# A selective scan on three engines: softplus of the next chunk in single steps, and five of sixteen input products moved to GpSimd

## The chip, the core and the metric

The kernel runs on one core of one Trainium2 chip. A core has five engines that run side by side, each with its own queue, worked through strictly in order: TensorE (matmul, PE in the profile; PEld is its weight load), VectorE (DVE), ScalarE (ACT), GpSimd (POOL) and SyncE (SP, which here issues most transfers). They share SBUF, the working memory of 128 partitions; TensorE writes its results to PSUM, which VectorE and ScalarE read and GpSimd does not in this kernel. The metric is device time in microseconds of one execution; lower is better. Before the change the median of three runs is 19478.2 us (19477.44 to 19488.43).

## What is computed

The reference is a two-layer network on an image of 4 × 64 × 64 positions with 128 channels. Only its first block matters here: a selective scan of an image in four directions (k = 0 to 3: by rows, by columns, and both reversed). Cut to that:

```python
x_dbl = einsum('bkdl,kcd->bkcl', xs, x_proj_weight)
dts, Bm, Cm = split(x_dbl, [R, R + N], axis=2)          # R = 8, N = 16 states
dts = einsum('bkrl,kdr->bkdl', dts, dt_projs_weight)
delta = softplus(dts + dt_projs_bias)                   # step sizes
A = -exp(A_logs)
def step(h, xs):                                        # over the 4096 positions
    ut, dt, bt, ct = xs
    dA = exp(dt[..., None] * A)
    h = dA * h + (dt * ut)[..., None] * bt[:, :, None, :]
    y = einsum('bkdn,bkn->bkd', h, ct)
    return (h, y)
```

There are 256 channels d (two halves h of 128, one channel to a partition), 16 states n, 4 directions k and 4 images b. All numbers are float32. After the scan come a normalization, a gate and a projection, then a mixture of experts, a second layer of mixing, and a long convolution by matmul.

## The kernel before

The images are worked one after the other. For each, a first part makes the convolved input xc and, by matmul, the rows of dts, B and C for all four directions, which go to a DRAM tensor xd. Then comes the scan, the part that the change touches, and then normalization and projection. Everything after the four images (experts, second layer, convolution) is not touched.

The scan of one image runs over 32 chunks: 4 directions of 8 chunks of 512 positions (SC). Directions 2 and 3 go backwards. In directions 1 and 3 (k odd) the image is read by columns, so that xc and the sum yac are accessed with a stride. In all there are 128 chunks, each like this:

- du = dl · xc (L296, VectorE, once for each half), into PSUM. dl holds the step sizes of this chunk. du has one buffer.
- For each of 16 states n: two transfers bring row n of B and of C from xd, spread over 128 partitions, into bb (L306) and cc (L310), six buffers each.
- For each half h of each state: ScalarE makes da = exp(dl · A) into PSUM (L315); VectorE makes the product db = du · bb (L319) and the scan hh from da and db (L323 backwards, L327 forwards); ScalarE copies the last column of hh to hst, with which the next chunk starts (L331); GpSimd makes hc = hh · cc (L333); TensorE adds hc to yps in PSUM by a matmul with the identity (L334; float32 takes two passes).
- At the end VectorE adds yps to yac (L338, once for each half).

The step sizes of the next chunk are made ahead, by step_sizes (L259 to L283), which is called once in a chunk, at n == 4 (L303). A transfer brings dts (L263). For each half a matmul makes dt_ps (L270), and ScalarE takes Abs of it (L274, into ex) and Relu (L275, into dl). Then for both halves at once, 1024 columns: ScalarE Exp (L276), VectorE w = ex + 1 (L277), VectorE ex = (w − 1) − ex (L279), ScalarE Ln (L280), GpSimd w − ex (L281) and dl + w (L282). Exp and Ln lie in different activation tables, so each chunk loads a table before Ln and one after it.

The tile that holds dt_ps carries the tag of da: both share the same two buffers in PSUM, in the order in which they are asked for. hh and hc have four buffers each, db two, dl two, ex and w one.

A framework places the instructions: it takes those of the program, orders each engine's queue by its own estimate, and puts in the semaphores. So the order in a queue isn't quite that of the program text. In the built kernel before, both dt_ps matmuls stand next to each other on TensorE, between the two sums of state 3, and Abs, Relu, Abs, Relu, Exp stand in one row on ScalarE.

Of the kernel before, what the change touches and what calls it, by code (L numbers as in the profile page):

```python
# [8 lines left out]
F32 = mybir.dt.float32  # L9
AF = mybir.ActivationFunctionType  # L10
ALU = mybir.AluOpType
# [4 lines left out]
P = 128  # L16
# [9 lines left out]
NCH = L // CH  # L26
SC = 512
NSC = L // SC
HALF = L // 2
TC = 512  # L30

# [2 lines left out]
def kernel(  # L34
# [35 lines left out]
    nc = tc.nc  # L70
# [53 lines left out]
    with ExitStack() as c0:  # L124
# [37 lines left out]
        for b in range(B):  # L162
# [5 lines left out]
            with tc.tile_pool(name="pa", bufs=1) as pa, tc.tile_pool(  # L168
                name="pa_ps", bufs=6, space=PSUM
# [23 lines left out]
                for g in range(8):  # L193
                    for h in range(2):
                        ps = pps.tile([P, 8, W], F32, name="cv_ps", tag="ps")
                        for t in range(9):
# [12 lines left out]
                            bias=cb[:, h : h + 1],  # L209
# [24 lines left out]
            with ExitStack() as cb_:  # L234
# [6 lines left out]
                with tc.tile_pool(name="pb", bufs=2) as pb, tc.tile_pool(  # L241
                    name="pb_ps", bufs=1, space=PSUM
                ) as bps:

                    chunks = []
                    for k in range(K):
                        for step in range(NSC):
                            chunks.append((k, step, NSC - 1 - step if k >= 2 else step))

                    def spatial(t, k, ci, h):  # L250

                        if k % 2 == 1:
                            n = SC // H
                            return t[:, h, :].rearrange("p (r w) -> p w r", w=W)[
                                :, ci * n : (ci + 1) * n, :
                            ]
                        return t[:, h, ci * SC : (ci + 1) * SC].rearrange("p (r w) -> p r w", w=W)

                    def step_sizes(k, ci):  # L259

                        cs = slice(ci * SC, (ci + 1) * SC)
                        dts = pb.tile([R, SC], F32, name="dts")
                        nc.sync.dma_start(dts, xd[k, 0:R, cs])  # L263
                        dl = pb.tile([P, 2, SC], F32, name="dl")
                        ex = pb.tile([P, 2, SC], F32, name="ex", bufs=1)
                        w = pb.tile([P, 2, SC], F32, name="w", bufs=1)

                        for h in range(2):
                            ps = bps.tile([P, SC], F32, name="dt_ps", tag="da", bufs=2)
                            nc.tensor.matmul(  # L270
                                ps, dtw[:, k, h * P : (h + 1) * P], dts, start=True, stop=True
                            )
                            bias = dtb[:, k, h : h + 1]
                            nc.scalar.activation(ex[:, h, :], ps, AF.Abs, bias=bias)  # L274
                            nc.scalar.activation(dl[:, h, :], ps, AF.Relu, bias=bias)  # L275
                        nc.scalar.activation(ex, ex, AF.Exp, scale=-1.0)  # L276
                        nc.vector.tensor_scalar(w, ex, 1.0, None, ALU.add)  # L277

                        nc.vector.scalar_tensor_tensor(ex, w, -1.0, ex, ALU.add, ALU.subtract)  # L279
                        nc.scalar.activation(w, w, AF.Ln)  # L280
                        nc.gpsimd.tensor_sub(w, w, ex)  # L281
                        nc.gpsimd.tensor_add(dl, dl, w)  # L282
                        return dl  # L283

                    ahead = step_sizes(chunks[0][0], chunks[0][2])
                    hst = None
                    for i, (k, step, ci) in enumerate(chunks):
                        rev = k >= 2
                        cs = slice(ci * SC, (ci + 1) * SC)
                        last = 0 if rev else SC - 1  # L290
                        if step == 0:
                            hst = pb.tile([P, 2, N], F32, name="hst")
                        dl = ahead
                        du = bps.tile([P, 2, SC], F32, name="du")
                        for h in range(2):
                            nc.vector.tensor_mul(  # L296
                                du[:, h, :].rearrange("p (r w) -> p r w", w=W),
                                dl[:, h, :].rearrange("p (r w) -> p r w", w=W),
                                spatial(xc, k, ci, h),
                            )  # L300
                        yps = bps.tile([P, 2, SC], F32, name="yps", bufs=2)
                        for n in range(N):
                            if n == 4 and i + 1 < len(chunks):  # L303
                                ahead = step_sizes(chunks[i + 1][0], chunks[i + 1][2])
                            bb = pb.tile([P, SC], F32, name="bb", bufs=6)
                            nc.sync.dma_start(  # L306
                                bb, xd[k, R + n : R + n + 1, cs].to_broadcast([P, SC])
                            )
                            cc = pb.tile([P, SC], F32, name="cc", bufs=6)
                            nc.sync.dma_start(  # L310
                                cc, xd[k, R + N + n : R + N + n + 1, cs].to_broadcast([P, SC])
                            )
                            for h in range(2):
                                da = bps.tile([P, SC], F32, name="da", tag="da", bufs=2)
                                nc.scalar.activation(  # L315
                                    da, dl[:, h, :], AF.Exp, scale=aneg[:, k, h, n : n + 1]
                                )
                                db = pb.tile([P, SC], F32, name="db")
                                nc.vector.tensor_mul(db, du[:, h, :], bb)  # L319
                                hh = pb.tile([P, SC], F32, name="hh", bufs=4)  # L320
                                init = 0.0 if step == 0 else hst[:, h, n : n + 1]
                                if rev:
                                    nc.vector.tensor_tensor_scan(  # L323
                                        hh[:, ::-1], da[:, ::-1], db[:, ::-1], init, ALU.mult, ALU.add
                                    )
                                else:
                                    nc.vector.tensor_tensor_scan(  # L327
                                        hh, da, db, init, ALU.mult, ALU.add
                                    )
                                if step < NSC - 1:  # L330
                                    nc.scalar.copy(hst[:, h, n : n + 1], hh[:, last : last + 1])  # L331
                                hc = pb.tile([P, SC], F32, name="hc", bufs=4)
                                nc.gpsimd.tensor_mul(hc, hh, cc)  # L333
                                nc.tensor.matmul(  # L334
                                    yps[:, h, :], ident, hc, start=(n == 0), stop=(n == N - 1)
                                )
                        for h in range(2):
                            nc.vector.tensor_add(  # L338
                                spatial(yac, k, ci, h),
                                spatial(yac, k, ci, h),  # L340
                                yps[:, h, :].rearrange("p (r w) -> p r w", w=W),
                            )


                with tc.tile_pool(name="po", bufs=2) as po, tc.tile_pool(
                    name="po_ps", bufs=2, space=PSUM
# [67 lines left out]
    with ExitStack() as c1:  # L414
# [11 lines left out]
        with ExitStack() as c2:  # L426
# [13 lines left out]
            with tc.tile_pool(name="gate", bufs=1) as gp, tc.tile_pool(  # L440
                name="gate_ps", bufs=4, space=PSUM
# [56 lines left out]
            with tc.tile_pool(name="exp", bufs=2) as ep, tc.tile_pool(  # L498
                name="exp_ps", bufs=2, space=PSUM
# [54 lines left out]
        with tc.tile_pool(name="l1", bufs=2) as lp, tc.tile_pool(  # L554
            name="l1_ps", bufs=6, space=PSUM
# [53 lines left out]
    with tc.tile_pool(name="stu_w", bufs=2) as wp:  # L609
# [38 lines left out]
        for src, acc in ((m_plus, accp), (m_minus, accm), (m_u, mu_t)):  # L648
            for i in range(4):
                n = src.shape[1]  # L650
# [17 lines left out]
    nc.vector.memset(carry, 0.0)  # L668
    for t in range(HALF // TC):
        nj = 4 * (t + 1)  # L670
# [32 lines left out]
        for k in range(KF):  # L703


            ev = fp.tile([P, HALF], F32, name="ev")
            nc.sync.dma_start(
                ev[:, 0:width],
                bass.AP(phi.tensor, phi[k, 0, HALF - width].offset, [[1, P], [1, width]]),
            )  # L710
            od = fp.tile([P, HALF + 1], F32, name="od")
            nc.sync.dma_start(
                od[:, 0 : width + 1],
                bass.AP(phi.tensor, phi[k, 1, HALF - width].offset, [[1, P], [1, width + 1]]),
            )
            for b in range(B):
                for a in range(2):
                    pe = fps.tile([P, TC], F32, name="e_ps", tag="eps")
                    po = fps.tile([P, TC], F32, name="o_ps", tag="ops")
                    for ps, slab, pa, off in ((pe, ev, a, 0), (po, od, 1 - a, 1 - a)):  # L720
                        for j in range(nj):
                            n = TC - max(0, P * (j - 4 * t))
# [46 lines left out]
def _layout(i):  # L769
# [15 lines left out]
    w2 = z["L0_ffn_weight2"]  # L785
    phi = np.zeros((KF, 2, HALF + P), f)
    for a in range(2):
# [52 lines left out]
```

## Time and profile before

| | us |
|---|---|
| median of three runs | 19478.2 |
| the profiled execution | 19460.9 |
| its span, first to last instruction | 19459.1 |
| VectorE busy in the span | 9714.3 (50%) |
| TensorE busy | 15393.0 (79%) |
| GpSimd busy | 5972.1 (31%) |
| ScalarE busy | 4733.9 (24%) |

The span has two very different halves. Up to about 10025 us the four images are scanned; after that TensorE alone sets the time. This can be seen in the page's rows of 40 slices (a digit is the busy share in tenths):

```profile
PE   6666676666766667666656699999999999999999
DVE  5999949999499995899983421111000000000000
POOL 3666626666266662666630000000000000000000
PEclk8888888888888888888885899999999999999999
```

Each image takes five slices; in four of them VectorE is at 9, and in the fifth, between two images, it falls to 4 or 5. In the groups of instructions (section 5 of the page) each row gives the line, the engine, the operation, out<-in with shapes and the count; then busy time in us and the mean in ns; then the idle time before them and what ended it. Instructions of an engine that follow each other overlap a little in these records, so that the distance from start to start, which the timeline shows, is some 0.06 to 0.1 us shorter than the duration.

The windows view gives the busy time of each engine in a stretch. For one chunk of direction 0 and one of direction 1:

```profile
651.50:718.90 67.40, 41.49 (x68) 12.16 (x68) 62.60 (x71) 31.98 (x72) 45.80 (x35) 0.87 0.51 126
992.90:1062.00 69.10, 42.70 (x68) 12.74 (x68) 64.30 (x71) 31.98 (x72) 46.10 (x35) 0.80 0.46 122
```

The columns are: the stretch and its length, then busy us (and instructions) of PE, PEld, DVE, ACT, POOL, then the granted clock of TensorE, the busy share of the DMA engines and GB/s.

### The profile page before, as it was taken

How to read it: one execution, taken by the hardware profiler on the slowest of the kernel's cores; microseconds unless marked ns; L12 is line 12 of the kernel's file. 1: busy time of each engine (PE TensorE's matmuls, PEld its weight loads, DVE VectorE, ACT ScalarE, POOL GpSimd, SP SyncE). 2: the span in 40 equal slices, each digit the busy share in tenths (PEclk: the TensorE clock that was granted, in tenths of full speed). 3: DMA queues.
4: the chain of work that ended last, by engine and by line, in shares of the span. 5: the costliest groups of instructions: out<-in, count | busy, mean ns of one | idle time of the engine just before them, and what ended most of it. 6: DMA issues, size and time to landing. Idle time of an engine off the chain costs nothing. (4 is left out here: it accounts for less than half of the span.)

```text
span 19459.1 us, 120106 instructions
## 1 busy us (share of the span) xinstructions
PE 15393.0 (79%) x36690; PEld 6691.3 (34%) x36690; DVE 9714.3 (50%) x10796; ACT 4733.9 (24%) x9696; POOL 5972.1 (31%) x4414
## 2 busy tenths in 40 slices
PE   6666676666766667666656699999999999999999
PEld 2111121111211112111126455555444444444444
DVE  5999949999499995899983421111000000000000
ACT  3444424444244442444431100000000000000000
POOL 3666626666266662666630000000000000000000
PEclk8888888888888888888885899999999999999999
DMA  3445414444144442344433100000000000000000
GB/s 76 125 124 126 117 58 124 122 124 122 53 125 124 126 123 59 119 123 123 125 88 95 45 11 20 11 11 19 12 10 10 10 21 9 9 11 11 9 9 11
DMA packets 733120, 1289.19 MB, mean 66 GB/s; under 512 B 75032, under 2 KB 175800, under 8 KB 728376
## 3 DMA queue, kind: packets, MB, share of 16 engines
q1 hardware_dynamic: 703864, 1245.85, 23.6%
q10 hardware_dynamic: 28608, 35.66, 0.6%
q8 instruction: 290, 4.75, 0.1%
q14 instruction: 358, 2.93, 0.1%
HBM read 1245.56 MB, written 35.65 MB: 66 GB/s over the span
## 5 line engine op out<-in xcount | busy, mean ns | idle before, releaser
L334 PE MATMUL yps<-hc,ident 128*128 128x512 f32 x8192 | 5191.1, 744 | 3355.9 <-POOL hc L333 3238.2
L333 POOL TENSOR_TENSOR hc<-hh,cc 128x512 f32<-128x512 f32 x4096 | 5285.6, 1312 | 2819.4 <-issue 1962.6
L334 PEld LDWEIGHTS yps<-hc,ident 128*128 128x128 f32 x8192 | 1534.2, 221 | 7007.4 <-POOL hc L333 6679.8
L723 PE MATMUL o_ps<-od,u 128*128 128x512 f32 (+3 forms) x10240 | 3828.8, 528 | 0.0
L723 PE MATMUL e_ps<-ev,u 128*128 128x512 f32 (+3 forms) x10240 | 3824.0, 528 | 0.0
L315 ACT ACTIVATE da<-dl,aneg 128x512 f32<-128x512 f32 x4096 | 2805.1, 688 | 587.7 <-DVE hh L323 290.8
L723 PEld LDWEIGHTS e_ps<-ev,u 128*128 128x128 f32 x10240 | 1945.2, 190 | 2119.5 <-issue 1837.0
L319 DVE TENSOR_TENSOR db<-du,bb 128x512 f32<-128x512 f32 x4096 | 2600.1, 673 | 8.7
L723 PEld LDWEIGHTS o_ps<-od,u 128*128 128x128 f32 x10240 | 1900.5, 190 | 1873.4 <-issue 1710.9
L732 ACT COPY es<-e_ps 128x512 f32<-128x512 f32 x512 | 299.6, 585 | 8015.5 <-PE e_ps L723 8015.5
L327 DVE TENSOR_TENSOR_SCAN hh<-da,hst,db 128x512 f32<-128x512 f32 x1792 | 2210.7, 1267 | 36.0 <-ACT da L315 36.0
L323 DVE TENSOR_TENSOR_SCAN hh<-da,hst,db 128x512 f32<-128x512 f32 x1792 | 2209.7, 1267 | 35.2 <-ACT da L315 34.7
L331 ACT COPY hst<-hh 128x1 f32<-128x1 f32 x3584 | 682.5, 190 | 3894.8 <-DVE hh L323 1958.9
L685 POOL COPY carry<-uT 128x2 f32<-128x2 f32 x16 | 3.0, 185 | 4964.3 <-ACT uT L684 4964.3
L277 DVE TENSOR_SCALAR w<-ex 128x1024 f32<-128x1024 f32 x128 | 93.9, 733 | 1201.3 <-ACT ex L276 668.9
L701 DVE TENSOR_TENSOR yacc<-yacc,y_ps 128x512 f32<-128x512 f32 x512 | 351.9, 687 | 526.4 <-PE y_ps L700 526.4
L699 PE MATMUL y_ps<-es,me 128*128 128x512 f32 x1024 | 524.1, 594 | 0.0
L198 PE MATMUL cv_ps<-xh,diag 128*128 128x512 f32 x1152 | 495.1, 592 | 0.0
L296 DVE TENSOR_TENSOR du<-dl,xc 128x512 f32<-128x512 f32 x256 | 359.6, 1405 | 28.3 <-POOL dl L282 23.8
L238 POOL TENSOR_SCALAR yac<-xc,dsum 128x4096 f32<-128x4096 f32 x8 | 86.5, 10824 | 878.3 <-DMA xd<-xd_st 878.3
L677 POOL COPY uT<-carry 128x2 f32<-128x2 f32 x16 | 3.0, 187 | 1045.5 <-DVE mo L663 943.7
L198 PEld LDWEIGHTS cv_ps<-xh,diag 128*128 128x128 f32 x1152 | 217.6, 189 | 276.9 <-issue 276.9
(1716 smaller groups left out, 7388.2 us busy)
## 6 DMA issues: line engine op xcount, KB each, us to landing
bb<-xd SPq DMA_DIRECT2D x2048, 256.0 KB
cc<-xd SPq DMA_DIRECT2D x2048, 256.0 KB
od<-in_phi_dram SPq DMA_DIRECT2D x16, 1024.5 KB
w1t<-in_w_dram SPq DMA_DIRECT2D x16, 1024.0 KB
w2t<-in_w_dram SPq DMA_DIRECT2D x64, 256.0 KB
ev<-in_phi_dram SPq DMA_DIRECT2D x16, 1024.0 KB
od<-in_phi_dram SPq DMA_DIRECT2D x16, 768.5 KB
ev<-in_phi_dram SPq DMA_DIRECT2D x16, 768.0 KB
```

What stands on the lines that cost most here:

```text
L198: nc.tensor.matmul(ps, diag[:, h, t, :], xh[:, h, 8 * g + dy : 8 * g + dy + 8, dx : dx + W], start=(t == 0), stop=(t == 8),)
L296: nc.vector.tensor_mul(du[:, h, :].rearrange("p (r w) -> p r w", w=W), dl[:, h, :].rearrange("p (r w) -> p r w", w=W), spatial(xc, k, ci, h),)
L315: nc.scalar.activation(da, dl[:, h, :], AF.Exp, scale=aneg[:, k, h, n : n + 1])
L319: nc.vector.tensor_mul(db, du[:, h, :], bb)
L323: nc.vector.tensor_tensor_scan(hh[:, ::-1], da[:, ::-1], db[:, ::-1], init, ALU.mult, ALU.add)
L327: nc.vector.tensor_tensor_scan(hh, da, db, init, ALU.mult, ALU.add)
L331: nc.scalar.copy(hst[:, h, n : n + 1], hh[:, last : last + 1])
L333: nc.gpsimd.tensor_mul(hc, hh, cc)
L334: nc.tensor.matmul(yps[:, h, :], ident, hc, start=(n == 0), stop=(n == N - 1))
L699: nc.tensor.matmul(ps, me[:, k, :], es, start=True, stop=False)
L701: nc.vector.tensor_add(yacc[:, b, a, :], yacc[:, b, a, :], ps)
L723: nc.tensor.matmul(ps[:, 0:n], u[:, b, 2 * j + pa, :], slab[:, P * j + off : P * j + off + n], start=(j == 0), stop=(j == nj - 1),)
```

## The change

Three things are altered.

1. step_sizes becomes a generator that stops after each piece: the matmul, Abs and Relu of one half; the same of the other half; Exp; the addition of 1; the subtraction on VectorE; Ln; the two operations of GpSimd, one by one. From n = 2 on, one piece is put between two states, so that the pieces stand in front of states 2 to 9 (and one more at the end that holds nothing).
2. The addition w = ex + 1 moves from VectorE to ScalarE (Identity with bias 1).
3. After du is made, ScalarE copies it to SBUF as dus (one buffer). For the states 2, 5, 8, 11 and 14 GpSimd makes db from dus and bb; for the others VectorE makes it from du as before. db gets four buffers instead of two.

```diff
+POOL_N = (2, 5, 8, 11, 14)
...
                             nc.scalar.activation(ex[:, h, :], ps, AF.Abs, bias=bias)
                             nc.scalar.activation(dl[:, h, :], ps, AF.Relu, bias=bias)
+                            yield None
                         nc.scalar.activation(ex, ex, AF.Exp, scale=-1.0)
-                        nc.vector.tensor_scalar(w, ex, 1.0, None, ALU.add)
+                        yield None
+                        nc.scalar.activation(w, ex, AF.Identity, bias=1.0)
+                        yield None
 
                         nc.vector.scalar_tensor_tensor(ex, w, -1.0, ex, ALU.add, ALU.subtract)
+                        yield None
                         nc.scalar.activation(w, w, AF.Ln)
+                        yield None
                         nc.gpsimd.tensor_sub(w, w, ex)
+                        yield None
                         nc.gpsimd.tensor_add(dl, dl, w)
-                        return dl
-
-                    ahead = step_sizes(chunks[0][0], chunks[0][2])
+                        yield dl
+
+                    def run(steps):
+                        got = None
+                        for got in steps:
+                            pass
+                        return got
+
+                    dl = run(step_sizes(chunks[0][0], chunks[0][2]))
...
-                        dl = ahead
                         du = bps.tile([P, 2, SC], F32, name="du")
+                        dus = pb.tile([P, 2, SC], F32, name="dus", bufs=1)
                         for h in range(2):
...
+                            nc.scalar.copy(dus[:, h, :], du[:, h, :])
                         yps = bps.tile([P, 2, SC], F32, name="yps", bufs=2)
+                        ahead = None
+                        if i + 1 < len(chunks):
+                            ahead = step_sizes(chunks[i + 1][0], chunks[i + 1][2])
+                        nxt = None
                         for n in range(N):
-                            if n == 4 and i + 1 < len(chunks):
-                                ahead = step_sizes(chunks[i + 1][0], chunks[i + 1][2])
+                            if ahead is not None and n >= 2:
+                                nxt = next(ahead, nxt)
...
-                                db = pb.tile([P, SC], F32, name="db")
-                                nc.vector.tensor_mul(db, du[:, h, :], bb)
+                                db = pb.tile([P, SC], F32, name="db", bufs=4)
+                                if n in POOL_N:
+                                    nc.gpsimd.tensor_mul(db, dus[:, h, :], bb)
+                                else:
+                                    nc.vector.tensor_mul(db, du[:, h, :], bb)
...
+                        dl = nxt
```

In the built kernel after the change, the queues stand like this at the head of a chunk (a number is the state, a and b its two halves; other instructions are left out):

```
TensorE  sum0a sum0b sum1a sum1b dt(first half) sum2a dt(second half) sum2b sum3a ...
GpSimd   hc0a hc0b db2a db2b hc1a hc1b hc2a hc2b hc3a db5a hc3b db5b hc4a hc4b hc5a w-ex hc5b dl+w hc6a hc6b db8a db8b hc7a ...
ScalarE  da1a da1b da2a Abs Relu da2b da3a Abs Relu da3b Exp da4a da4b Identity da5a da5b (table) Ln (table) da6a ...
VectorE  db0a db0b scan0a scan0b db1a db1b scan1a scan1b db3a db3b scan2a db4a scan2b db4b scan3a scan3b scan4a ...
```

At the end of a chunk VectorE has: the last scans of state 15, du of the next chunk twice, yac twice, then db0a and db0b of the next chunk. Before the change one db stood between du and yac.

## Prediction

> **What bounds the kernel now.** I read four things, in this order: the busy rows of the page, the windows by stage, the costliest groups, and the timelines of four engines over one chunk. The chain that ended last is no help: it lies in the last 9,434 us, where TensorE is busy for 9,000 us. The change touches only the four scan stretches (about 230–2430, 2780–4965, 5300–7490, 7830–10025 us). Their groups, from the page:
>
> ```profile
> L334 PE MATMUL yps<-hc,ident 128*128 128x512 f32 x8192 | 5191.1, 744 | 3355.9 <-POOL hc L333 3238.2
> L333 POOL TENSOR_TENSOR hc<-hh,cc 128x512 f32<-128x512 f32 x4096 | 5285.6, 1312 | 2819.4 <-issue 1962.6
> ...
> L319 DVE TENSOR_TENSOR db<-du,bb 128x512 f32<-128x512 f32 x4096 | 2600.1, 673 | 8.7
> ...
> L327 DVE TENSOR_TENSOR_SCAN hh<-da,hst,db 128x512 f32<-128x512 f32 x1792 | 2210.7, 1267 | 36.0 <-ACT da L315 36.0
> ```
>
> VectorE hardly waits before its products (8.7 us) and scans (36.0 us); GpSimd and TensorE wait thousands. VectorE sets the pace. In the windows view one chunk, 651.5 to 718.9 us, has VectorE busy 62.60 of 67.40 us, GpSimd 45.80, ScalarE 31.98. VectorE's timeline of that chunk:
>
> ```profile
> 660.68 1.26 DVE L319 TENSOR_TENSOR db<-du,bb 128x512 f32<-128x512 f32 x2
> 661.86 2.45 DVE L327 TENSOR_TENSOR_SCAN hh<-da,hst,db 128x512 f32<-128x512 f32 x2
> ...
> 674.98 0.69 DVE L277 TENSOR_SCALAR w<-ex 128x1024 f32<-128x1024 f32 x1 [4.03 <-ACT ex L276]
> ...
> 682.26 1.28 DVE L327 TENSOR_TENSOR_SCAN hh<-da,hst,db 128x512 f32<-128x512 f32 x1 [0.67 <-ACT da L315]
> ...
> 718.92 2.53 DVE L296 TENSOR_TENSOR du<-dl,xc 128x512 f32<-128x512 f32 x2
> ...
> 723.05 1.29 DVE L338 TENSOR_TENSOR yac<-yac,yps 128x512 f32<-128x512 f32 x2 [0.89 <-PE yps L334]
> ```
>
> By start times a pair of products (both halves of one state) takes 1.18 us and a pair of scans 2.37, so a state takes 3.55. The only large hole is the softplus (4.03 + 0.67). From one du to the next, 651.55 to 718.92, the chunk is 67.4 us; where k is odd (L277 at 948.97 and at 1018.10) it is 69.1. Mean 68.25, over 128 chunks. GpSimd's timeline and TensorE's:
>
> ```profile
> 677.04 2.10 POOL L333 TENSOR_TENSOR hc<-hh,cc 128x512 f32<-128x512 f32 x1 [5.41 <-issue]
> 679.37 1.27 POOL L333 TENSOR_TENSOR hc<-hh,cc 128x512 f32<-128x512 f32 x1 [0.22 <-DVE hh L327]
> 680.60 2.35 POOL L281 TENSOR_TENSOR w<-w,ex 128x1024 f32<-128x1024 f32 x1
> 683.03 2.35 POOL L282 TENSOR_TENSOR dl<-dl,w 128x1024 f32<-128x1024 f32 x1
> 685.33 7.39 POOL L333 TENSOR_TENSOR hc<-hh,cc 128x512 f32<-128x512 f32 x6
> ```
>
> ```profile
> 653.57 1.12 PE L334 MATMUL yps<-hc,ident 128*128 128x512 f32 x2 [0.54 <-POOL hc L333]
> 658.67 2.08 PE L334 MATMUL yps<-hc,ident 128*128 128x512 f32 x2 [3.97 <-POOL hc L333]
> ...
> 670.42 1.98 PE L270 MATMUL dt_ps<-dts,dtw 8*128 8x512 f32 x4
> ```
>
> Six GpSimd products in a row last 7.39 us, so each step is (7.39 − 1.27)/5 = 1.225. The product at 677.04 lasted 2.10 instead of 1.27, beside VectorE's L279 (676.83, 1.20 us), whose two inputs are both in SBUF: 0.83 us lost. The pair at 650.59 lasted 2.93 instead of 2.49, beside du (L296, two SBUF inputs as well): 0.44 lost; for odd k a pair lasted 3.30 (922.28): 0.81 lost. TensorE's two passes for one product take 1.12 us, but 2.08 after 3.97 us of idleness; there the granted clock was 0.50 (658.6–662.6), then 0.98.
>
> **The change, part by part, in us per chunk.**
>
> VectorE: ten products go (5 × 1.18 = 5.9) and L277 goes (0.65 by start times). If its softplus holes closed too (4.7), it would need 67.4 − 5.9 − 0.65 − 4.7 = 56.1.
>
> GpSimd: 42 products instead of 32, 42 × 1.225 = 51.4; softplus's two operations 2 × 2.35 = 4.7; collisions with L279 0.8 and with both du (now GpSimd still has products queued when they run) 2 × 0.44 = 0.9. Sum 57.8; for odd k 2 × 0.81 gives 58.5. An SBUF-by-SBUF product with dus stands nowhere in the trace; its nearest row is hc, of the same shape and place: 1.225 as a step in a run, 1.312 as the mean with collisions. I take 1.225; the other end adds 10 × 0.09 = 0.9. So GpSimd now has more to do than VectorE, and sets the pace; each time it stops counts. The row speaks against the move as such: it buys 5.9 us on one engine for 12.3 on the other.
>
> The Trainium skill (GPSIMD Engine Reference, 4.1 Engine selection) says the same more sharply: elementwise work on two inputs belongs on VectorE, since GpSimd is about twice as slow; by that ratio, an estimate, a product would step at 2 × 0.59 = 1.18 in place of 1.225, and the sum would be 42 × 0.045 = 1.9 us less.
>
> ScalarE gains Identity (as L276: 1.07) and two copies of du (between 0.585, the copy out of PSUM at L227, and 0.69, the activations of the same size): 2.4. It is busy 32 of 67.4, so I put this at nothing; without that cover Identity alone would hold back state 5's da by 0.95. SP issues the same transfers; dts comes a chunk earlier, hidden in a queue of 0.3 us issues. dus has one buffer, so its copy waits for state 14's product of the chunk before, which in the walk below ends some 5 us earlier: nothing. Splitting the softplus adds no instruction; its VectorE and GpSimd operations are counted above.
>
> Now the stops. I walked one chunk along the built order of each engine, letting each instruction start when its engine and its inputs were ready.
>
> Stop 1, at the chunk's end. GpSimd runs some 3 us behind VectorE there, so the sum into yac must wait for the last hc; nothing else for GpSimd is ready until the next chunk's first scan. Last hc → TensorE pair 1.15 → two yac 1.2 (2.3 for odd k: 927.64 to 929.93) → two db 1.18 → scan 1.27 → handovers 0.3: 5.1 (odd 6.2). The same hole exists today, but GpSimd's time is not what counts today.
>
> Stop 2, the first half of the softplus. dt_ps takes one of the two PSUM buffers of da. In TensorE's order the first dt stands behind state 1's second hc, and state 2's second da can be written only when Abs and Relu have read dt. GpSimd meanwhile does six products (hc0, hc0, db2, db2, hc1, hc1) and then hc2's first half, 1.225, before it runs dry. From the end of hc1: TensorE pair 1.12, dt to Abs 1.16 (670.42 to 671.58), Abs and Relu 0.58 + 0.69, state copy and da 0.8, scan 1.27, handovers 0.2 = 5.8; less 1.2 is 4.6. Before this, TensorE has idled over 5 us at stop 1, so it may be at half clock: the pair then takes 0.95 more and dt about 0.85 more (estimate, the same ratio). Ends 0 and 1.8; I take 0.9, since in the trace half clock ended 4 us after the restart in this chunk but later for odd k (granted clock 0.55 in 934–940, restart 932.66), and dt comes 7 to 8 us after it. Stop 2: 5.5. Queued behind the waiting instructions are, on TensorE, every later sum, on ScalarE the state copies and the next da, on VectorE the scans of states 2 to 4: nothing else can feed GpSimd.
>
> The Trainium skill (TensorE: Matmul & The Clock Gate, Part 1: The HAM clock gate) halves the rate after an idle window of about 3.4 us and restores it after one busy window as long; by that rule dt would run at full rate, and the sum would be 0.9 less.
>
> Late products of GpSimd also make VectorE wait before the scans of states 8, 11 and 14, up to 1.6 us; that costs nothing while GpSimd is the slower one.
>
> Stop 3: the second dt holds the other buffer. hc2's second half to hc3: copy, da, scan, handover 0.1 + 0.69 + 1.27 + 0.1 = 2.16, less 1.225: 0.9.
>
> Sum: 57.8 + 5.1 + 5.5 + 0.9 = 69.3; odd 58.5 + 6.2 + 5.5 + 0.9 = 71.1. Mean 70.2 against 68.25: +1.95 × 128 = +250. Against the profiled execution's 19,460.9 that is 19,711; the median of the runs shown lies 17.3 above it, so 19,728. **Forecast: 19,730 us**; own range 19,610 (no half clock, −115) to 19,960 (half clock throughout, +115, and the dearer product, +115).
>
> **Rivals.**
>
> *GpSimd stays fed (faster).* If dt did not wait behind late hc matmuls, stops 2 and 3 would vanish: 62.9 and 64.7, mean 63.8, −4.45 × 128 = −570, 18,910. For: today dt starts right after its neighbours (670.42). Against: today GpSimd is hardly behind there, while the new order puts two db in front of hc1. It decides from the point where stop 2 is under 3.5 us. 0.13.
>
> *No change.* Stops shorter by 2 us in all: 19,480. Nothing favours just that. 0.05.
>
> *TensorE becomes a bound at the chunk's head (slower still).* At half clock its pair takes 2.08 against GpSimd's 1.225, so for the first five states it falls behind, dt waits the full 1.8, and a late pair or two adds about 1 us: 72.1, +3.85 × 128 = +493, 19,970. For: half clock in every chunk shown after such a hole. Against: it ended within 7 us. 0.20.
>
> *VectorE bound* (the change does just what its words say, no stop counts): 56.1, 12.15 × 128 = 1,560 less. GpSimd's 57.8 alone rules this out; it gets no share.
>
> **Numbers.** Forecast 0.62, the others 0.20, 0.13, 0.05. Range 19,540 to 19,990. This kernel's measurement can tell about 0.2% (39 us) from nothing. Faster 0.13, within 0.2% 0.05, slower 0.82.
>
> **What would show it.** GpSimd busy about 57 of 70 us in a chunk, with two holes of 5 us or more, one before hc of state 0, one within state 2. VectorE waiting 4 to 6 us for da in state 2 and about 4 us for yps before yac, and L277 gone. Chunk period 69.3 and 71.1. If GpSimd's holes in state 2 are below 3 us, or VectorE's busy time is above GpSimd's, I am wrong.

## The result, and the profile after

The changed kernel takes 19,742.7 us (median of 4 runs, 19,737.2 to 19,746.5) against 19,482.0 for the kernel before (4 runs on the same chip): ratio 1.0133, 95% interval 1.0116 to 1.0151. It is slower by some 260 us. The profiled execution of it has a span of 19,744.7 us, 285.6 above that of before. All of this lies in the scan stretches: from the first chunk's du to the last chunk's it is 9,994.7 us after against 9,703.7 before (+291.0). The mean distance from one chunk's du to the next one's, over the 124 distances that lie inside a stretch, grew from 67.97 to 70.47 us.

From the page of the changed kernel, its clock row and groups (columns as before):

```profile
PEclk8777787777877777777776799999999999999999
...
L357 PE MATMUL yps<-hc,ident 128*128 128x512 f32 x8192 | 5776.5, 821 | 2948.1 <-POOL hc L356 2801.3
L356 POOL TENSOR_TENSOR hc<-hh,cc 128x512 f32<-128x512 f32 x4096 | 5209.4, 1302 | 1683.3 <-issue 957.6
...
L350 DVE TENSOR_TENSOR_SCAN hh<-da,hst,db 128x512 f32<-128x512 f32 x1792 | 2218.3, 1273 | 568.7 <-ACT da L335 398.5
...
L340 POOL TENSOR_TENSOR db<-dus,bb 128x512 f32<-128x512 f32 x1280 | 1603.1, 1271 | 0.0
...
L311 DVE TENSOR_TENSOR du<-dl,xc 128x512 f32<-128x512 f32 x256 | 600.2, 2345 | 153.3 <-ACT dus L316 92.4
```

The scans, which hardly waited before (36.0 us for this line), now wait 568.7 us, mostly for da. GpSimd's idle time before hc fell from 2,819 to 1,683 us, but it did not vanish, although there are now 42 products in each chunk. A product with dus takes 1,271 ns, as a plain hc does, so the operation that the trace before did not show has the price taken for it. du takes 2,345 ns in place of 1,405. TensorE's clock row shows 7 in most of the slices where it showed 8, and the sums got longer (821 instead of 744 ns).

The windows view, two chunks of direction 0 from du to du, and then a piece of the second (columns: stretch, length, busy us of PE, PEld, DVE, ACT, POOL, granted clock, DMA share, GB/s):

```profile
388.50:457.00 68.50, 45.23 (x68) 12.45 (x68) 58.62 (x60) 34.02 (x76) 57.17 (x45) 0.81 0.51 122
597.90:669.40 71.50, 49.82 (x69) 14.22 (x69) 58.80 (x61) 34.05 (x75) 57.26 (x45) 0.76 0.53 118
612.50:624.00 11.50, 9.79 (x10) 2.62 (x10) 4.84 (x6) 3.45 (x9) 4.61 (x4) 0.50 0.44 87
```

GpSimd is busy for 57.2 us in both, VectorE for 58.7; neither is full. The chunks differ by 3.0 us at the same work. GpSimd's timeline of the two (start, duration, operation, count, and in brackets the idle time before and what ended it) shows where:

```profile
398.18 2.49 POOL L356 TENSOR_TENSOR hc<-hh,cc 128x512 f32<-128x512 f32 x2 [5.68 <-issue]
...
411.31 1.27 POOL L356 TENSOR_TENSOR hc<-hh,cc 128x512 f32<-128x512 f32 x1 [4.52 <-DVE hh L350]
413.51 1.26 POOL L356 TENSOR_TENSOR hc<-hh,cc 128x512 f32<-128x512 f32 x1 [0.93 <-issue]
...
593.63 7.38 POOL L356 TENSOR_TENSOR hc<-hh,cc 128x512 f32<-128x512 f32 x6
607.24 2.49 POOL L356 TENSOR_TENSOR hc<-hh,cc 128x512 f32<-128x512 f32 x2 [6.22 <-issue]
...
622.74 1.27 POOL L356 TENSOR_TENSOR hc<-hh,cc 128x512 f32<-128x512 f32 x1 [6.89 <-DVE hh L350]
624.94 1.26 POOL L356 TENSOR_TENSOR hc<-hh,cc 128x512 f32<-128x512 f32 x1 [0.92 <-issue]
629.84 3.48 POOL L356 TENSOR_TENSOR hc<-hh,cc 128x512 f32<-128x512 f32 x2
633.52 1.27 POOL L356 TENSOR_TENSOR hc<-hh,cc 128x512 f32<-128x512 f32 x1 [0.20 <-issue]
```

These are the three stops of the prediction. With a last 0.20 us (after L285), the short chunk is 57.17 + 5.68 + 4.52 + 0.93 + 0.20 = 68.5, the long one 57.26 + 6.22 + 6.89 + 0.92 + 0.20 = 71.5: the chunk is GpSimd's work plus GpSimd's stops, with nothing left over. TensorE's timeline tells why stop 2 is 4.52 in one and 6.89 in the other:

```profile
404.40 2.35 PE L357 MATMUL yps<-hc,ident 128*128 128x512 f32 x4 [1.15 <-POOL hc L356]
406.69 1.12 PE L273 MATMUL dt_ps<-dts,dtw 8*128 8x512 f32 x2
...
608.55 3.78 PE L357 MATMUL yps<-hc,ident 128*128 128x512 f32 x4 [5.16 <-POOL hc L356]
613.46 3.78 PE L357 MATMUL yps<-hc,ident 128*128 128x512 f32 x4 [1.12 <-POOL hc L356]
617.16 2.07 PE L273 MATMUL dt_ps<-dts,dtw 8*128 8x512 f32 x2
```

In both, the first dt starts the moment the sums of state 1 are through: it stands behind them. In the long chunk those sums take 3.78 us instead of 2.35 and dt 2.07 instead of 1.12, together 2.4 us, the difference of the two stops; the granted clock there was 0.50. VectorE's timeline of the long chunk, from the end of the chunk before it to state 2's second scan and to L285, and ScalarE's at the first dt:

```profile
597.86 3.71 DVE L311 TENSOR_TENSOR du<-dl,xc 128x512 f32<-128x512 f32 x1
602.27 0.70 DVE L311 TENSOR_TENSOR du<-dl,xc 128x512 f32<-128x512 f32 x1 [0.71 <-ACT dus L316]
603.42 1.29 DVE L362 TENSOR_TENSOR yac<-yac,yps 128x512 f32<-128x512 f32 x2 [0.45 <-PE yps L357]
...
621.31 1.28 DVE L350 TENSOR_TENSOR_SCAN hh<-da,hst,db 128x512 f32<-128x512 f32 x1 [6.40 <-ACT da L335]
...
630.88 1.31 DVE L285 SCALAR_TENSOR_TENSOR ex<-w,ex 128x1024 f32<-128x1024 f32 x1
```

```profile
619.27 0.69 ACT L277 ACTIVATE ex<-dt_ps,dtb 128x512 f32<-128x512 f32 x1 [6.63 <-PE dt_ps L273]
```

The first half of du lasts 3.71 us, its second half 0.70: the first ends 0.56 us after the last of GpSimd's six products (593.63 to 601.01), and I read this as du held off by them. Then the second half waits 0.71 us for the copy of the first.

### The profile page after: what moved, and what is told of

Same layout as the page of the kernel before. It is cut to its first block, busy times and chain, and to the rows that moved or that the text cites. A ratio compares the mean times of both kernels' runs of the same rounds, so it can differ in the third digit from the quotient of the medians.

```text
span 19744.7 us, 119458 instructions
## 1 busy us (share of the span) xinstructions
PE 16053.6 (81%) x36690; PEld 6825.4 (35%) x36690; DVE 9182.3 (47%) x9388; ACT 5000.4 (25%) x10080; POOL 7421.1 (38%) x5694
## 5 line engine op out<-in xcount | busy, mean ns | idle before, releaser
L357 PE MATMUL yps<-hc,ident 128*128 128x512 f32 x8192 | 5776.5, 821 | 2948.1 <-POOL hc L356 2801.3
L356 POOL TENSOR_TENSOR hc<-hh,cc 128x512 f32<-128x512 f32 x4096 | 5209.4, 1302 | 1683.3 <-issue 957.6
L357 PEld LDWEIGHTS yps<-hc,ident 128*128 128x128 f32 x8192 | 1679.4, 239 | 7015.4 <-POOL hc L356 6496.4
L350 DVE TENSOR_TENSOR_SCAN hh<-da,hst,db 128x512 f32<-128x512 f32 x1792 | 2218.3, 1273 | 568.7 <-ACT da L335 398.5
L342 DVE TENSOR_TENSOR db<-du,bb 128x512 f32<-128x512 f32 x2816 | 1834.8, 675 | 11.2 <-ACT dus L316 2.6
L340 POOL TENSOR_TENSOR db<-dus,bb 128x512 f32<-128x512 f32 x1280 | 1603.1, 1271 | 0.0
L311 DVE TENSOR_TENSOR du<-dl,xc 128x512 f32<-128x512 f32 x256 | 600.2, 2345 | 153.3 <-ACT dus L316 92.4
L285 DVE SCALAR_TENSOR_TENSOR ex<-w,ex 128x1024 f32<-128x1024 f32 x128 | 179.6, 1403 | 714.7 <-ACT w L282 357.6
L273 PE MATMUL dt_ps<-dts,dtw 8*128 8x512 f32 x512 | 357.3, 784 | 54.2 <-ACT dl L278 30.2
```

The costliest lines, as they stand in the source:

```text
L311: nc.vector.tensor_mul(du[:, h, :].rearrange("p (r w) -> p r w", w=W), dl[:, h, :].rearrange("p (r w) -> p r w", w=W), spatial(xc, k, ci, h),)
L340: nc.gpsimd.tensor_mul(db, dus[:, h, :], bb)
L350: nc.vector.tensor_tensor_scan(hh, da, db, init, ALU.mult, ALU.add)
L357: nc.tensor.matmul(yps[:, h, :], ident, hc, start=(n == 0), stop=(n == N - 1))
```

## The experiments

Times are medians, each beside runs of the kernel before on the same chip (19,475 to 19,479). "A" is the prediction's account, GpSimd's pace plus its stops.

**The two halves of the change.** First the steps without the products on GpSimd:

```diff
-POOL_N = (2, 5, 8, 11, 14)
+POOL_N = ()
...
-                        dus = pb.tile([P, 2, SC], F32, name="dus", bufs=1)
...
-                            nc.scalar.copy(dus[:, h, :], du[:, h, :])
```

> The softplus in single steps alone: all 16 states' products stay on VectorE, no dus. Theory A (GpSimd sets the pace after the change, and stands still at the chunk's end and in state 2, where dt_ps waits behind late sums and holds a buffer of da): without the ten products GpSimd has slack again, dt comes soon after state 1, VectorE is the bound at 62 us of work plus 1 to 3 of waiting in state 2; chunk 63 to 65 (k odd 64.6 to 66.6), that is 3.5 x 128 = 450 below before: 18,910 to 19,170. Theory B (the load of 42 GpSimd products with its collisions is the whole loss, the place of the softplus has no part in it): the same sign, also about 19,000. Theory C (TensorE's half clock is the loss): stops and half clock remain, 19,400 or more.

19,081.3 us, ratio 0.9796 (0.9782 to 0.9811). Then the products on GpSimd, with softplus in one block in front of state 4 and L277 on VectorE, as before:

```diff
-                            if ahead is not None and n >= 2:
-                                nxt = next(ahead, nxt)
+                            if n == 4 and i + 1 < len(chunks):
+                                ahead = step_sizes(chunks[i + 1][0], chunks[i + 1][2])
```

> The five states on GpSimd alone, softplus in one block at n = 4 with its addition on VectorE as before. Theory A: GpSimd's 57 us of work plus the chunk's end 6 and one long hole around the block of softplus: chunk 67.7 to 69.0 (k odd 69.3 to 70.6), 0 to 1.5 above before: 19,490 to 19,680. Theory B: the same loss as the full change or more, since the softplus holes stay: 19,740 or above.

19,582.0 us, ratio 1.0055 (1.0038 to 1.0072). Alone, the steps gain 398 us and the products lose 103; a sum of the two would be a gain of 295, and together they lose 261. So some 556 us are neither's own: they come from the two meeting.

**dt_ps in buffers of its own.** The change with dt_ps in two PSUM buffers that it does not share with da; yps gives up its second tile to make room.

```diff
-                            ps = bps.tile([P, SC], F32, name="dt_ps", tag="da", bufs=2)
+                            ps = bps.tile([P, SC], F32, name="dt_ps", bufs=2)
...
-                        yps = bps.tile([P, 2, SC], F32, name="yps", bufs=2)
+                        yps = bps.tile([P, 2, SC], F32, name="yps")
```

> The full change, but dt_ps has two PSUM buffers of its own; yps gives up its second one for it. Theory A: the hole of GpSimd in state 2 (4.5 to 6.9) and the 0.9 after it vanish, chunk about 60.5 for both kinds, 7.7 x 128 = 990 below before: 18,400 to 18,600. Theory B: GpSimd's load is unchanged, so about 19,700, at most 100 less. Theory C: 19,500 to 19,700, since dt waits no longer but the clock is as before.

18,562.9 us, ratio 0.9528 (0.9514 to 0.9542). GpSimd's timeline at a chunk's head, behind the six products of the chunk before:

```profile
624.28 2.35 POOL L289 TENSOR_TENSOR w<-w,ex 128x1024 f32<-128x1024 f32 x1 [4.27 <-ACT w L287]
626.71 2.34 POOL L291 TENSOR_TENSOR dl<-dl,w 128x1024 f32<-128x1024 f32 x1
629.01 2.49 POOL L356 TENSOR_TENSOR hc<-hh,cc 128x512 f32<-128x512 f32 x2
```

From here to the next chunk's end nothing stands in brackets: one stop of 4.27 us is left, for Ln, and 56.15 busy us make the chunk of 60.5. Stops 2 and 3 are gone. The run changes two things at once, though: with free buffers the softplus is also built in an earlier place, the first dt in front of the last state's sums and GpSimd's two operations (L289, L291) in front of state 0's first hc, where the change has them beside hc of state 5. And one yps tile might have done it. The yps tile alone:

> The change with one yps tile in place of two and nothing else. It is the control for the two runs that took yps's second tile away to make room in PSUM (the softplus's dt_ps in buffers of its own, and the added matmuls at the chunk's end). Theory A (the gain of those runs came from dt_ps's own buffers, and from TensorE being kept busy): the second yps tile is not needed, since the next chunk's first matmul into yps comes some 5 us after the last sum out of it; 19,700 to 19,785, as the change itself (19,743). Theory D (one yps tile is itself worth something, by the order that it makes): under 19,650, or above 19,840.

19,734.3 us, ratio 1.0135 (1.0118 to 1.0152): it is worth nothing (8 us beside the change).

**The place of dt, with the shared buffers.** The softplus's steps begin at another state, the buffers stay:

```diff
-                            if ahead is not None and n >= 2:
+                            if ahead is not None and n >= 0:
```

> The change with the softplus's steps begun at state 0 in place of state 2, dt_ps still in da's two PSUM buffers. In the built order the first dt now stands before the last state's sums of the chunk before, and the second one behind them, so neither stands behind a state's late sums with the next da waiting for it. Theory A (what costs is that dt stands on TensorE behind sums whose hc is late while da waits for its buffer): 65.0 and 66.5 us a chunk by a walk along the built order, against 68.5 and 70.2 for the change by the same walk, 3.6 x 128 = 460 less: 19,150 to 19,350, below before. Rival (two producers in two buffers cost the same wherever dt stands): 19,650 or more.

19,170.6 us, ratio 0.9844 (0.9829 to 0.9858). TensorE's timeline and GpSimd's:

```profile
638.87 5.40 PE L357 MATMUL yps<-hc,ident 128*128 128x512 f32 x8 [2.55 <-POOL hc L356]
644.19 1.12 PE L273 MATMUL dt_ps<-dts,dtw 8*128 8x512 f32 x2
645.24 1.98 PE L357 MATMUL yps<-hc,ident 128*128 128x512 f32 x4
651.00 2.07 PE L273 MATMUL dt_ps<-dts,dtw 8*128 8x512 f32 x2 [3.77 <-DVE hh L350]
```

```profile
651.07 2.49 POOL L356 TENSOR_TENSOR hc<-hh,cc 128x512 f32<-128x512 f32 x2 [6.13 <-issue]
...
663.92 1.26 POOL L356 TENSOR_TENSOR hc<-hh,cc 128x512 f32<-128x512 f32 x1 [2.41 <-issue]
```

dt now has the place that it has in the run with own buffers, one half before the last state's sums and one behind them. The earlier place, with the buffers still shared, gives 19,742.7 − 19,170.6 = 572 us. Sharing still costs: the second dt waits 3.77 us for a scan to free a da buffer; GpSimd stops for 6.13 us at the chunk's end, as in the change, and then for 0.54 and 2.41 us. From there to own buffers (19,170.6 − 18,562.9) it is another 608 us. Not all of that is shown to be the buffers': the steps behind dt stand earlier there as well, and no run has own buffers with the steps where the change has them. With `n >= 7`, far behind the chunk's head:

> The change with the softplus's steps begun at state 7 in place of state 2, dt_ps still in da's two PSUM buffers. dt again stands behind a state's sums, but seven states after the stop at the chunk's end, when GpSimd has worked through a longer row and TensorE has been busy for 20 us and more. Theory A: the stop in the middle stays, at full clock and shorter: 65.5 and 67.2 us a chunk by the walk, 3.0 x 128 = 390 less, 19,250 to 19,450. Rival (the stop is as long wherever in the chunk it is, since GpSimd always runs the same distance behind): 19,600 to 19,750; half clock alone would explain 19,510.

19,268.9 us, ratio 0.9893 (0.9878 to 0.9908). GpSimd's timeline has the stop in the middle again, as 0.26 + 1.64 + 1.05 us, each wait for something else (the 0.26, at 614.47, for a transfer of cc):

```profile
617.38 2.50 POOL L356 TENSOR_TENSOR hc<-hh,cc 128x512 f32<-128x512 f32 x2 [1.64 <-PE yps L357]
620.92 1.26 POOL L356 TENSOR_TENSOR hc<-hh,cc 128x512 f32<-128x512 f32 x1 [1.05 <-DVE hh L350]
```

That is 2.95 in place of stops 2 and 3 of the change (5.45 to 7.8): with the same shared buffers the stop depends on where dt stands. That it is GpSimd's lag there which counts, and not the clock, was not separated.

**Own buffers without products on GpSimd.** It completes a table of two by two:

```diff
-POOL_N = (2, 5, 8, 11, 14)
+POOL_N = ()
...
-                            ps = bps.tile([P, SC], F32, name="dt_ps", tag="da", bufs=2)
+                            ps = bps.tile([P, SC], F32, name="dt_ps", bufs=2)
...
+                            dtp.append(ps)
+                        yield None
```

(Both matmuls form a first piece, which runs ahead of state 0; yps has one tile, and there is no copy of du.)

> The softplus in single steps with dt_ps in two PSUM buffers of its own, no product db on GpSimd and no copy of du. Theory A (the shared da/dt_ps buffers cost time only because GpSimd, with 42 products, is late with the sums in front of dt): without those products GpSimd is not late, so own buffers add nothing to the single steps alone (19,081): 19,040 to 19,140, and the five GpSimd states are then worth some 500 to 550 less with own buffers (18,563) where they cost 660 more with shared ones (19,743 against 19,081). Theory E (the sharing costs the same whatever GpSimd does, 19,743 - 18,563 = 1,180): about 17,900. Theory B (products on GpSimd cost VectorE more by collisions than they save): under 18,560.

18,920.4 us, ratio 0.9718 (0.9703 to 0.9732).

```
us                       dt_ps shares da's buffers    dt_ps has its own
no product on GpSimd             19,081                   18,920
five states on GpSimd            19,743                   18,563
```

The right column has more than other buffers: in both of its runs the whole softplus is built in front of state 0's first hc. The interval expected, 19,040 to 19,140, was missed by 120: own buffers, with the order that they allow, are worth 161 us also without GpSimd's load. The groups of the steps-only run and of this one, a scan line of each, show it; the waits of this line and of its sister for the other direction, 92.6 + 89.7 us, fall to 19.9 + 15.9, which is 146 of the 161:

```profile
L348 DVE TENSOR_TENSOR_SCAN hh<-da,hst,db 128x512 f32<-128x512 f32 x1792 | 2205.1, 1266 | 92.6 <-ACT da L333 80.2
```

```profile
L355 DVE TENSOR_TENSOR_SCAN hh<-da,hst,db 128x512 f32<-128x512 f32 x1792 | 2199.7, 1264 | 19.9 <-ACT da L340 19.6
```

But the main reading stands: own buffers are worth 161 us beside a GpSimd with room and 1,180 beside a loaded one, and the five states lose 661 us in the one case and gain 358 in the other. That products on GpSimd cost more by collisions than they save is refuted.

**The half clock.** At the chunk's end TensorE gets four more matmuls of the last hc, into a bank that nothing reads, so that it doesn't idle:

```diff
+                        if i + 1 < len(chunks):
+                            hot = bps.tile([P, SC], F32, name="hot")
+                            for q in range(4):
+                                nc.tensor.matmul(hot, ident, hc, start=True, stop=True)
```

> The full change plus four matmuls of the last hc into a spare PSUM bank at each chunk's end, whose result nothing reads; yps has one buffer. They fill TensorE's idle 5 us there. Theory A: the clock is full when dt comes, so every chunk is one of the short ones (68.5, k odd 70.2) instead of 68.6 or 71.5 by turns: about 1.2 x 128 = 150 less than the change, 19,590, still above before. Theory C: well below before, under 19,450. If the clock has no part in it: 19,740.

19,508.9 us (10 runs), ratio 1.0016 (1.0006 to 1.0025), between the two forecasts: still above the kernel before, as A asked, but the gain beside the same kernel without the matmuls (19,734.3) is 225 us and not 150. Not all of it is the clock's, since the built order changed as well: the first dt now stands behind the sums of state 0 and the second behind those of state 1, each earlier than in the change. TensorE's timeline and GpSimd's:

```profile
603.85 2.36 PE L357 MATMUL yps<-hc,ident 128*128 128x512 f32 x4 [1.73 <-POOL hc L356]
606.14 1.12 PE L273 MATMUL dt_ps<-dts,dtw 8*128 8x512 f32 x2
608.76 3.30 PE L357 MATMUL yps<-hc,ident 128*128 128x512 f32 x4 [1.50 <-POOL hc L356]
611.99 2.07 PE L273 MATMUL dt_ps<-dts,dtw 8*128 8x512 f32 x2
```

```profile
611.54 1.26 POOL L356 TENSOR_TENSOR hc<-hh,cc 128x512 f32<-128x512 f32 x1 [0.39 <-DVE hh L350]
617.55 1.26 POOL L356 TENSOR_TENSOR hc<-hh,cc 128x512 f32<-128x512 f32 x1 [4.74 <-issue]
```

The first dt is at full rate, the second one again at half, and GpSimd's long stop has moved from the first dt to the second: 0.39 and 4.74 us in place of 4.52 and 0.93. How much of the 225 us is the clock and how much the place stays open. Both together are not why the gain of own buffers is missing: that, 1,180 us, is five times as much.

**The copies of du.** Both halves of du first, then both copies:

```diff
                                 spatial(xc, k, ci, h),
                             )
+                        for h in range(2):
                             nc.scalar.copy(dus[:, h, :], du[:, h, :])
```

> The change with both halves of du made first and both copies of du to dus after them, so that du's second half no longer stands behind the copy of the first (0.71 us in the changed kernel's profile). Theory A (the stop at the chunk's end is a chain on which du stands): 0.7 us x 128 = 90 less, 19,620 to 19,690. Rival (du's second half is hidden by GpSimd's own wait, and the copies come later for state 2's product): 19,743 within 30.

19,672.1 us, ratio 1.0104 (1.0089 to 1.0119): 71 us less, near the 90 expected. du's second half stood on the chain that sets the chunk.

**How many states.** With own buffers and one yps tile, first four states and the copies behind both du, then the five of the change with the same copies, then three with the copies as in the change:

```diff
-POOL_N = (2, 5, 8, 11, 14)
+POOL_N = (2, 6, 10, 14)
```

> dt_ps in two PSUM buffers of its own, one yps tile, both halves of du before both copies, and four states on GpSimd (2, 6, 10, 14) in place of five. Theory A (with the stops in state 2 gone GpSimd's own 57.8 us and the chunk's end set the pace; one state less takes 2 x 1.225 = 2.45 from GpSimd and gives VectorE 1.18, which has room): 58.4 us a chunk by a walk along the built order, (58.4 - 68.25) x 128 = -1,260, 18,150 to 18,400. Rival (what is left is VectorE's, so a state taken back costs its 1.18 us): 18,563 + 150 = 18,710.

18,288.8 us, ratio 0.9394 (0.938 to 0.9408).

> dt_ps in two PSUM buffers of its own, one yps tile, both halves of du before both copies, and the change's five states on GpSimd; beside the run with four of them (18,289) it prices the fifth state, beside the run with the copies between (18,563) it prices the copies' place. Theory A (with five GpSimd is the bound, so the fifth state costs its 2.45 us a chunk less what VectorE gains): 18,480 to 18,600. Rival (the copies' place made the gain): 18,250 to 18,330.

18,395.8 us, ratio 0.9444 (0.943 to 0.9458).

> dt_ps in two PSUM buffers of its own, one yps tile, copies as in the change, and three states on GpSimd (3, 7, 11). By the walk 58.4 and 60.1 us a chunk, against 57.6 and 59.2 for four states with the copies behind: VectorE now sets the pace and gets 1.18 us of a state back. Theory A: 18,289 + 0.85 x 128 = 18,400, within 60. Rival (GpSimd would still be the bound): below 18,289.

18,401.5 us, ratio 0.9449 (0.9433 to 0.9465).

The step from 18,563 to 18,289 thus has two parts: the copies' place, 167 us, and the fifth state, 107 us. Neither of the two readings put before the five-state run was right alone. With three or five states it is some 110 us slower than with four, though the three-state run has the copies in the other place. Four states, own buffers and late copies are 6.1% faster than the kernel before and 7.4% faster than the change. GpSimd's timeline of it at a chunk's end, and VectorE's there:

```profile
599.47 7.83 POOL L357 TENSOR_TENSOR hc<-hh,cc 128x512 f32<-128x512 f32 x6
609.55 2.35 POOL L289 TENSOR_TENSOR w<-w,ex 128x1024 f32<-128x1024 f32 x1 [2.25 <-ACT w L287]
...
627.18 2.50 POOL L357 TENSOR_TENSOR hc<-hh,cc 128x512 f32<-128x512 f32 x2 [0.60 <-PE yps L358]
```

```profile
604.97 1.22 DVE L311 TENSOR_TENSOR du<-dl,xc 128x512 f32<-128x512 f32 x1
...
616.33 2.46 DVE L351 TENSOR_TENSOR_SCAN hh<-da,hst,db 128x512 f32<-128x512 f32 x2 [1.03 <-ACT da L336]
```

GpSimd has small stops in the middle again (0.60), so it is no longer the one that is always behind; VectorE's waits in this stretch come to little more than 1 us, and du takes 1.22 us, not 3.71. In the windows view of the chunk before (546.3 to 605.0 us) VectorE is busy for 57.23 of 58.70 us and GpSimd for 54.31: VectorE is the fuller one now.

## Why the prediction was right, point by point

- **GpSimd sets the pace, 57.8 us (odd 58.5).** The mechanism holds: busy time plus stops make each chunk. Measured 57.2 in nearly every chunk. The product with dus costs what hc costs, and the collision beside L285 is there (two hc in 3.48 at 629.84, 0.98 us lost; I had 0.8). The term mis-sized is the collision with du, 0.9 and 1.6: GpSimd lost nothing there. VectorE did, by 3 us, and it came back in stop 1.
- **Stop 1, 5.1 (odd 6.2).** Measured 5.68 and 6.22, and 7.45 in a chunk of odd k (at 1031.74). The chain that I followed began with the last hc; in fact it begins with du, which ends only when GpSimd's row is done. So the wait of yac for yps, which I named as a sign at about 4 us, was 0.45: what waits is du.
- **Stop 2, 5.5, from dt in da's buffers.** The mechanism holds to the instruction: dt behind state 1's sums, ScalarE's timeline has 6.63 us without work until dt, da for state 2's second scan 6.40 us late. 4.52 measured at full clock, where I had 4.6. The half clock, 0 to 1.8 with 0.9 taken, was 2.4 where it struck, since both of state 1's sums ran slow and not one pair; 26 of the 64 even chunks inside a stretch were long ones, which makes 1.0 on average.
- **Stop 3, 0.9.** 0.92.
- **The sum.** 69.3 forecast for even chunks (k even), which came as 68.5 or 71.5 and 69.51 on average; 71.1 for odd ones, 71.50 on average. By averages the even chunk is 57.04 of work, 5.93, 5.44 and 1.08 of stops (the last with the 0.20), the odd one 57.24, 7.29, 5.86 and 1.10: the work was put 0.8 and 1.3 us too high and stop 1 0.8 and 1.1 too low, so that these two errors nearly cancel. That is luck, as is part of the closeness of 19,743 to 19,730. The distance before was taken as 68.25, from two chunks, and is 67.97 over all, so the growth was 2.50 us a chunk, not 1.95; 19 us came back between the images (the three distances from du to du that span a change of image are 1,256 us together, 1,275 before), and the span grew by 286. The medians differ by 261, since the execution profiled before lay 21 us under its median and the one after 4 above; the working said 250.
- **ScalarE's additions at nothing.** Wrong for the copies: the first one stood between du's halves, and moving the copies behind both halves gave 71 us here and 167 with own buffers. The cover that I named, ScalarE's idle time, is no cover for a reader that has to wait its turn behind the copy.
- **The rivals.** That GpSimd stays fed if dt doesn't wait was a true mechanism, and own buffers show its size: 18,563, beyond the 18,910 given. GpSimd's 57.8 + 5.1 became 56.15 + 4.27: neither du nor L285 lengthens its products there, and the one stop that is left is shorter. The half clock as a brake at the chunk's head happened in the long chunks, without making TensorE the bound. VectorE bound: excluded by GpSimd's 57 us, and near to true in the four-state version, where it is busy for 57.23 of 58.7 us.

## What to carry to other kernels

Before moving work to an engine that runs behind another, look up which results of it stand in front of unrelated work in a strictly ordered queue: here 12 us of products made each sum late, and the softplus's first matmul, queued behind the sums, then stopped three engines because its PSUM buffer was da's. Two producers that take turns in one pair of buffers are tied to each other's lag; give them buffers of their own first, and count the load afterwards, since the best of the shares tried (four states of 16) was found with the stops gone; with shared buffers only none and five were tried.

## What the hardware showed that I had not expected

A product of two SBUF operands on VectorE did not take turns with GpSimd's ready products here. du was free to start at 597.86 in the changed kernel, and ended at 601.57; its second half takes 0.70, so it may have started near 600.9 (an estimate), when GpSimd's row of six ended at 601.01. At least two of GpSimd's products were started while du waited. The Trainium skill (SBUF — State Buffer, Who interferes with whom) says that a VectorE instruction with two SBUF inputs contends with GpSimd's reads, and, where it speaks of VectorE's two-port modes, that whoever issues first gets the shared ports for the whole instruction. If that holds for du too, it would wait for one product, at most 1.27 us (an estimate from the trace's duration), and the trace shows more than twice as much. L285, also with two inputs in SBUF, got between two products at 630.88 and delayed GpSimd by 0.98 us, and in the four-state run du itself took only 1.22 us while GpSimd's row of six took 7.83 instead of 7.38. So both orders occur, and what decides was not settled.

TensorE kept the half clock through unbroken work. In the long chunk its matmuls run without a gap from 613.46 to 623.24, after state 0's two sums at 608.55, and the granted clock from 612.5 to 624.0 was 0.50; in the short chunk it was 0.55 in the four microseconds after the restart at 399.50, and 0.96 in the seven after that. The Trainium skill (TensorE: Matmul & The Clock Gate, Part 1: The HAM clock gate) restores full rate after one busy window of about 3.4 us; the short chunk agrees, the long one does not. The matmuls are of the same kind in both, so their two passes alone do not explain it. That even chunks of the same program come out at either 68.5 or 71.5 us is shown; why is open.
